# Three of four relus of the second mixture on ScalarE

## The chip, the cores and the metric

The kernel runs on one NeuronCore of a Trainium2 chip. A core has five engines that each work through a list of their own, in order: TensorE (PE in the profile, with its weight loads as PEld), VectorE (DVE), ScalarE (ACT), GpSimd (POOL) and SyncE (SP, which here issues DMAs). They wait for one another by semaphores. The metric is the device time of one execution in microseconds (us). Three runs of the kernel before gave 2256.85, 2263.62 and 2266.39 us, median 2263.62.

## The reference

For 32 sequences of 64 tokens with 256 channels, a first layer (a gated mixture of nine experts and a hyperbolic attention) is added to x. A second layer follows: the "second mixture" of dense networks named cond2, an attention with rotary positions, and a routed mixture of four experts. All is float32. The part that matters here, cut down:

```python
def _dense(x, wi_, wo_):
    return relu(x @ wi_) @ wo_
s0 = _dense(x, swi[0], swo[0])
s1 = _dense(x, swi[1], swo[1])
h  = relu(einsum('bsd,bdf->bsf', x, wi[type_label]))
eo = einsum('bsf,bfd->bsd', h, wo[type_label])
w  = softmax(relu(concat(eo[:,0], s0[:,0], s1[:,0]) @ g1) @ g2)
return eo * w[:,0] + s0 * w[:,1] + s1 * w[:,2]
```

Each token passes three dense networks of 256 to 1024 to 256, two shared and one chosen by the label of its sequence, and each of the three has a relu over its 1024 hidden values.

## The kernel before

The tokens are sorted into 16 tiles of 128, two tiles to a group, so there are eight groups. The first mixture takes the first part of the kernel. Then a loop `for k in range(1, GROUPS + 1)` (L1441) runs eight steps. Step k holds up to three pieces of work, written as Python generators and interleaved by `woven` (L1426): the hyperbolic attention of group k ("h", L396), the second mixture of group k-1 ("s", `selected`, L901), and the gate, rotary attention and routing of group k-2 ("r", L1322). The last step has the first weights of the routed mixture in place of "h". The routed mixture itself follows.

`woven` sets the order in which the instructions are written. The framework's planner then arranges them on each engine by its own estimate of when inputs are due, so a change of the engine of one instruction can also change the order of others. Once built, the order of every engine's list is fixed and it is kept at run time.

In `selected`, `dense` (L908) does four rounds: four matmuls of 128x256 (L917) fill one 128x512 bank of PSUM (`ph`, three buffers), and `relu` (L862) writes it to SBUF as `h`. Then sixteen matmuls (L931) bring the four `h` down to 256 channels. Each group runs this for the two shared networks. The chosen one is a third `dense` in groups 3 to 7, which hold one label each; in groups 0 to 2 it is made tile by tile, with two relus for each of two tiles (matmuls L969, transposes L984, matmuls L995). So every group has three fours of relus, 12 in all, and eight groups have 96.

`relu` counts its calls in `n_relu`. Odd calls run as an ACTIVATE on ScalarE (L866), even ones as a `tensor_scalar` maximum on VectorE (L868). In the first step (`first_step`) all twelve run on ScalarE.

Other lines that the prediction's steps touch:

- `hyperbolic`: exponentials L424 and L425, `u` L454, its transposes L294, keys `kb` L299, the scores L310, L464 and L465, square root L469, L472, logarithm L473, square L475, the mask L334.
- `attend`: row maxima L345, the subtraction on GpSimd L346, the exponential L347, transposes L354 with copies L356 (ScalarE) and L358 (VectorE), the product with the values L365, its sums L373, `y` L377, transposes L386, the copy L388, the output product L392.
- `gated_sum`: L1033, L1041, L1045, L1049, L1052, L1063, L1075, and the weighted sum L1082 to L1084.
- `rotary`: statistics L1096 and L1098, square root L1099, normalised rows `xn` L1102, transposes L1118, `pad` L1120, convolution `hc` L1132 and L1134, projection L267 and L270.
- SyncE's list: weights into `slot` (L875, L879), values into `vb` (L283).

Exponential, square root, logarithm and the gate of the first mixture need different function tables on ScalarE; each switch is an ACT_TABLE_LOAD in its list.

Of the kernel before, what the change touches and what calls it, by code (L numbers as in the profile page):

```python
# [76 lines left out]
def adaln_attn_ffn_kernel(ctx: ExitStack, tc: tile.TileContext, a, consts, out):  # L77
# [779 lines left out]
    n_relu = 0  # L857


    first_step = False  # L860

    def relu(dst, src):  # L862
        nonlocal n_relu
        n_relu += 1
        if n_relu % 2 or first_step:
            nc.scalar.activation(dst, src, AF.Relu)  # L866
        else:
            nc.vector.tensor_scalar(dst, src, 0.0, None, ALU.max)  # L868
# [32 lines left out]
    def selected(g, xT):  # L901
# [6 lines left out]
        def dense(w):  # L908

            hs = []  # L910
            for half in range(2):
                for pair in range(2):
                    ph = busy([P, 2, GN])
                    for k in range(2):
                        for c in range(2):
                            fc = 2 * pair + k
                            nc.tensor.matmul(  # L917
                                ph[:, k, :],
                                lhsT=w[half][:, c, fc * P : (fc + 1) * P],
                                rhs=xT[:, c, :],  # L920
                                start=c == 0,
                                stop=c == 1,
                            )
                    h = hidden([P, 2, GN])
                    relu(h, ph)
                    hs.append(h)
                    yield
# [31 lines left out]
        for k in range(NG if g < MIXED + PAIRS else 0):  # L959
# [5 lines left out]
            for half in range(2):  # L965
                ph = busy([P, 512])
                for c in range(2):
                    for b2 in range(P // width):
                        nc.tensor.matmul(  # L969
                            ph[b2 * width : (b2 + 1) * width, :],  # L970
                            lhsT=xT[:, c, k * P + b2 * width : k * P + (b2 + 1) * width],
                            rhs=w[b2][half][:, c, :],
                            start=c == 0,
                            stop=c == 1,
                        )
                h = hidden([P, 512])
                relu(h, ph)
                hs.append(h)
                yield
# [461 lines left out]
    for k in range(1, GROUPS + 1):  # L1441
# [11 lines left out]
        first_step = k == 1  # L1453
# [176 lines left out]
```

## Time and profile before

| | |
|---|---|
| three runs, median (us) | 2263.62 |
| the profiled execution's own time (us) | 2267.08 |
| its span, first to last instruction (us) | 2265.3 |
| PE busy in the span | 98% |
| DVE, ACT, POOL busy | 59%, 34%, 35% |
| mean granted TensorE clock | 0.994 |
| relus on ScalarE (L866), mean ns | 54, 590 |
| relus on VectorE (L868), mean ns | 42, 685 |
| first and last relu start (us from the span's start) | 1357.3, 2007.5 |

The profile names groups of instructions by their line, engine and tiles (out<-in). A group's row gives its busy time, the mean of one instruction in ns, and the idle time of the engine before them with what ended it. A row of the list of waits gives who waited, for whom, the total in us, how often, and the longest. A row of a table by stretches gives the busy time of each engine between two times and the clock that was granted to TensorE. A row of the timeline gives start, duration, engine, line, operation, and in square brackets the idle time before it and what ended it.

### The profile page before, as it was taken

The numbers are of one execution on the slowest core, as the hardware profiler recorded it, in microseconds if no ns is written. First come the engines' busy times: TensorE is split into PE (matmuls) and PEld (weight loads), VectorE is DVE, ScalarE is ACT, GpSimd is POOL, SyncE is SP. The second block draws the span as 40 slices with busy tenths as digits, with TensorE's granted clock in tenths as the row PEclk, the third lists the DMA queues.
The fourth block names the chain that finished last, engine by engine and source line by source line (L and its number), as shares of the span: only waits on it lengthen the run. The fifth ranks groups of instructions, "written<-read, shape, count | busy, mean of one in ns | idle before, by whom it ended". The sixth has DMA issues, their size and how long they took to land. (4 is left out here: it accounts for less than half of the span.)

```text
span 2265.3 us, 29780 instructions
## 1 busy us (share of the span) xinstructions
PE 2208.9 (98%) x11224; PEld 1801.3 (80%) x11224; DVE 1332.4 (59%) x2470; ACT 777.2 (34%) x1244; POOL 797.8 (35%) x693
## 2 busy tenths in 40 slices
PE   7999999999999999999999999999999999999998
PEld 6888888888888888888888786677687777766665
DVE  7465575565655756547565755767668668545222
ACT  2333333333333333333333544445245245222111
POOL 5653444454443545445354441122121221111110
PEclk9999999999999999999999999999999999999999
DMA  4010010190100101001000026443332322531110
GB/s 125 31 37 20 1 38 19 41 329 1 38 19 4 54 1 38 19 1 56 1 19 8 6 79 202 140 122 92 112 95 82 106 81 82 200 133 32 40 38 24
DMA packets 101470, 145.16 MB, mean 64 GB/s; under 512 B 10246, under 2 KB 63696, under 8 KB 101328
## 3 DMA queue, kind: packets, MB, share of 16 engines
q1 hardware_dynamic: 93056, 130.43, 18.0%
q0 software_dynamic: 3488, 10.00, 1.3%
q10 hardware_dynamic: 4784, 2.83, 0.4%
q8 instruction: 90, 1.47, 0.3%
q14 instruction: 52, 0.43, 0.1%
HBM read 114.67 MB, written 24.29 MB: 61 GB/s over the span
## 5 line engine op out<-in xcount | busy, mean ns | idle before, releaser
L677 ACT COPY cp<-X 128x512 f32<-128x512 f32 x432 | 251.3, 586 | 527.0 <-PE X L665 523.7
L685 DVE TENSOR_TENSOR cp<-W,cp 128x512 f32<-128x512 f32 x272 | 186.4, 690 | 86.2 <-ACT cp L677 71.4
L718 POOL TENSOR_TENSOR h_t<-h_t,h_b 128x512 f32<-128x512 f32 x72 | 95.0, 1319 | 349.0 <-DVE h_t L687 348.9
L686 ACT ACTIVATE cp<-cp 128x512 f32<-128x512 f32 x216 | 136.3, 631 | 226.3 <-DVE cp L685 226.2
L792 POOL TENSOR_TENSOR xg<-xT,mixw 128x1024 f32<-128x1024 f32 x36 | 71.2, 1978 | 325.9 <-PE W L665 309.2
L917 PE MATMUL ph<-xT,slot 128*128 128x256 f32 x672 | 167.4, 395 | 0.0
L931 PE MATMUL ph<-slot,h 128*128 128x256 f32 x672 | 161.0, 383 | 0.0
L685 DVE TENSOR_TENSOR cp<-Y,cp 128x512 f32<-128x512 f32 x160 | 109.9, 689 | 84.7 <-PE Y L665 77.0
L687 DVE TENSOR_TENSOR h_b<-cp 128x512 f32<-128x512 f32 x144 | 139.9, 972 | 19.3 <-ACT cp L686 3.3
L665 PE MATMUL X<-gS,w 128*128 128x256 f32 x576 | 148.1, 379 | 0.0
L665 PE MATMUL X<-xS,w 128*128 128x256 f32 x576 | 148.1, 380 | 0.0
L917 PEld LDWEIGHTS ph<-xT,slot 128*128 128x128 f32 x672 | 128.3, 197 | 16.9
L639 DVE TENSOR_TENSOR condT<-downA,condT 128x256 f32<-128x256 f32 x132 | 55.2, 419 | 141.3 <-PE downA L628 141.1
L931 PEld LDWEIGHTS ph<-slot,h 128*128 128x128 f32 x672 | 124.3, 191 | 16.3 <-issue 0.6
L628 PE MATMUL downA<-h_t,w 128*128 128x256 f32 x576 | 136.1, 379 | 0.0
L665 PEld LDWEIGHTS X<-gS,w 128*128 128x128 f32 x576 | 109.2, 190 | 15.4 <-issue 0.6
L628 PEld LDWEIGHTS downA<-h_t,w 128*128 128x128 f32 x576 | 109.4, 190 | 14.8
L665 PEld LDWEIGHTS X<-xS,w 128*128 128x128 f32 x576 | 109.0, 190 | 15.2 <-ACT cp L677 0.5
L639 DVE TENSOR_TENSOR condT<-downB,condT 128x256 f32<-128x256 f32 x104 | 43.4, 417 | 123.3 <-PE downB L628 123.3
L721 POOL TENSOR_TENSOR h_t<-h_b,h_t 128x512 f32<-128x512 f32 x72 | 111.5, 1549 | 0.0
L719 POOL TENSOR_TENSOR h_t<-h_b,h_t 128x512 f32<-128x512 f32 x72 | 105.2, 1461 | 4.2
L720 POOL TENSOR_TENSOR h_t<-h_b,h_t 128x512 f32<-128x512 f32 x72 | 95.7, 1329 | 0.0
(405 smaller groups left out, 4592.3 us busy)
## 6 DMA issues: line engine op xcount, KB each, us to landing
rows_d<-blank SPq DMA_DIRECT2D x67, 258.0 KB
slot<-in_L_cond_swi SPq DMA_DIRECT2D x32, 512.0 KB
slot<-in_L_cond_swo SPq DMA_DIRECT2D x32, 512.0 KB
slot<-in_L_cond_wi SPq DMA_DIRECT2D x26, 512.0 KB
slot<-in_L_cond_wo SPq DMA_DIRECT2D x26, 512.0 KB
w<-in_L_cond_Wg SPq DMA_DIRECT2D x8, 1024.0 KB
w<-in_L_cond_Wu SPq DMA_DIRECT2D x8, 1024.0 KB
w<-in_L_cond_Wd SPq DMA_DIRECT2D x8, 1024.0 KB
```

The costliest lines, as they stand in the source:

```text
L628: nc.tensor.matmul(po, lhsT=wd[l](q), rhs=h[q // 2][r][:, q % 2, :], start=fresh and q == 0, stop=q == Q - 1, skip_group_check=True,)
L639: nc.vector.tensor_tensor(acc, po, acc, ALU.add)
L665: nc.tensor.matmul(bank[m, name][:, k, :], lhsT=w[l][:, q * P : (q + 1) * P], rhs=src[r], start=fresh and k == 0, stop=True, skip_group_ch ...
L677: nc.scalar.copy(side[m, name], bank[m, "X"])
L685: nc.vector.tensor_tensor(t, bank[m, b], t, ALU.add)
L686: nc.scalar.activation(side["g", name], side["g", name], AF.Silu)
L687: nc.vector.tensor_tensor(h[key], side["g", name], side["u", name], ALU.mult)
L719: nc.gpsimd.tensor_tensor(h["t2"], h["b22"], h["t1"], ALU.subtract)
L720: nc.gpsimd.tensor_tensor(h["t3"], h["b22"], b12, ALU.subtract)
L721: nc.gpsimd.tensor_tensor(h["t4"], h["b21"], h["t2"], ALU.subtract)
L917: nc.tensor.matmul(ph[:, k, :], lhsT=w[half][:, c, fc * P : (fc + 1) * P], rhs=xT[:, c, :], start=c == 0, stop=c == 1,)
L931: nc.tensor.matmul(po[:, k, :], lhsT=hs[fc // 2][:, fc % 2, k * P : (k + 1) * P], rhs=w[2 + fc // 4][:, fc % 4, :], start=fc == 0, stop=fc ...
```

## The change

`n_relu % 2` becomes `n_relu % 4`. A call runs on VectorE only if its number divides by four and the first step is over.

```diff
     def relu(dst, src):
         nonlocal n_relu
         n_relu += 1
-        if n_relu % 2 or first_step:
+        if n_relu % 4 or first_step:
             nc.scalar.activation(dst, src, AF.Relu)
         else:
             nc.vector.tensor_scalar(dst, src, 0.0, None, ALU.max)
```

Each group makes twelve calls, so the count starts every group at a multiple of four: of each four, the second moves from VectorE to ScalarE, the fourth stays on VectorE. The first step has no relu on VectorE before or after. In the other seven steps 3 x 7 = 21 relus move: ScalarE has 75 and VectorE 21, where they had 54 and 42. Nothing else in the source changes. The planner arranges the lists of PE, VectorE and ScalarE anew around the moved relus; GpSimd's list stays the same, and SyncE's has one weight load and one register load in other places.

## The prediction

> **What bounds the kernel now.** I read the page's first part, then the groups by shape, the waits of PE, a table by stretches, and the timeline of step k = 5.
>
> ```profile
> span 2265.3 us, 29780 instructions
> ...
> PE 2208.9 (98%) x11224; PEld 1801.3 (80%) x11224; DVE 1332.4 (59%) x2470; ACT 777.2 (34%) x1244; POOL 797.8 (35%) x693
> ```
>
> PE is busy all but 2265.3 - 2208.9 = 56.4 us. The change touches no matmul, so time can only come from PE's idle time, or from its clock. The relus run from 1357 to 2008 us; in the stretch 1350 to 2010 PE is busy 634.28 of 660 us, so 25.7 us of idle time are at stake, and that includes step 1, which the change leaves alone.
>
> ```profile
> L866 ACT ACTIVATE h<-ph 128x512 f32<-128x512 f32 x54 | 31.8, 590 | 67.1 <-PE ph L917 49.9 <-PE ph L969 17.2
> ...
> L868 DVE TENSOR_SCALAR h<-ph 128x512 f32<-128x512 f32 x42 | 28.8, 685 | 15.3 <-PE ph L917 10.8 <-PE ph L969 4.4
> ```
>
> Both kinds of relu wait for PE. In the answers for these two lines, the waits of anyone for a relu sum to 1.3 us. The relus themselves are not late. What counts is what stands behind them on each engine. PE's own waits in steps 2 to 7 (1400 to 2000 us):
>
> ```profile
> PE at L267 <- DVE hc L1134: 6.2, 7, 0.9
> PE pt L354 <- ACT s L347: 5.3, 6, 0.9
> PE ph L1049 <- ACT h L1045: 2.1, 4, 0.6
> PE ph L1033 <- DMA vb<-v: 1.7, 2, 1.0
> PE pt L386 <- DVE y L377: 1.6, 4, 0.4
> ```
>
> The first is the end of a chain on VectorE, the second of one on ScalarE. They are nearly equal: the change takes from one and adds to the other. By stretches (columns: busy PE, PEld, DVE, ACT, POOL, then granted clock, DMA share, GB/s):
>
> ```profile
> 1510.00:1520.00 10.00, 8.45 (x42) 5.44 (x41) 5.72 (x16) 2.07 (x4) 2.07 (x2) 0.97 0.43 129
> 1520.00:1530.00 10.00, 10.00 (x45) 8.59 (x45) 7.58 (x37) 3.67 (x9) 0.00 (x0) 0.86 0.21 59
> 1600.00:1610.00 10.00, 8.17 (x38) 5.24 (x38) 5.87 (x17) 2.61 (x7) 2.07 (x2) 0.91 0.47 133
> 1610.00:1620.00 10.00, 10.00 (x32) 8.38 (x32) 4.97 (x26) 0.95 (x3) 0.00 (x0) 0.58 0.07 8
> 1640.00:1650.00 10.00, 10.00 (x68) 7.31 (x66) 9.73 (x17) 9.45 (x12) 1.53 (x2) 1.00 0.23 68
> ```
>
> Two things: in the middle of a step (last row) VectorE and ScalarE are both full, so ScalarE's 34% over the span says nothing there. And after stretches in which PE idled 1.55 and 1.83 us of ten, the clock fell, to 0.86 and 0.58.
>
> **The change, part by part.** 21 relus move. VectorE loses 21 x 685 = 14.4 us, ScalarE gains 21 x 590 = 12.4 us. On the end of the kernel only the place counts; there are three, each seven times. The built lists give the new order.
>
> *First four, near the start of the step.* VectorE in step 5:
>
> ```profile
> 1701.71 0.68 DVE L868 TENSOR_SCALAR h<-ph 128x512 f32<-128x512 f32 x1
> 1702.31 0.15 DVE L1076 TENSOR_REDUCE red<-wgt 128x2 f32<-128x6 f32 x1
> ```
>
> The next instruction starts 0.60 us later, and VectorE then has hardly a gap up to `xn` (L1102), whose transposes lead to `pad`, `hc` and PE's wait at L267:
>
> ```profile
> 1710.03 0.33 PE L1118 MATMUL pt<-ident,xn 128*128 128x128 f32 x1 [0.23 <-DVE xn L1102]
> ...
> 1714.60 1.98 PE L267 MATMUL at<-w_qkv,hc 128*128 128x512 f32 x4 [0.89 <-DVE hc L1134]
> ```
>
> So `hc` comes 0.60 us earlier. But the new list of PE puts 17 matmuls of the mixture between L1063 and this L267 (apart from the first twelve) where there were 18, in steps 2, 5, 6, 7; one is 0.43 us (eight records of L931 from 1710.96 to 1712.69, two to a matmul), and it has to be made up later. Net gain 0.60 - 0.43 = 0.17 each. In step 4 it is 12 in place of 14: 0.60 - 0.86 = -0.26. In steps 3 and 8 the count stays: 0.60 each. Together 4 x 0.17 - 0.26 + 2 x 0.60 = 1.6 us gained. On ScalarE this relu now stands ahead of the second exponential (L425): it starts when its matmuls end, near 1701.7, so L425 ends near 1702.5 where it ended at 1701.28. VectorE asks for it at 1706.79 (L444): hidden by 4 us of other VectorE work; without that cover 1.2 us a step.
>
> *Second four, inside the full stretch.* The relu goes in ScalarE's list ahead of the logarithm's table load, where a relu takes 0.48 us (first two rows, start to start):
>
> ```profile
> 1733.56 0.58 ACT L866 ACTIVATE h<-ph 128x512 f32<-128x512 f32 x1
> 1734.04 1.04 ACT L475 ACTIVATE za<-za 128x1024 f32<-128x1024 f32 x1
> 1736.62 0.59 ACT L356 COPY sT<-pt 128x512 f32<-128x512 f32 x1 [1.53 <-PE pt L354]
> ```
>
> The 1.53 us gap ahead of L356 takes it up: nothing. The mask (L334) that waits for the square has been put later in VectorE's list. VectorE's keys (L299) may start 0.6 us earlier; PE shows no wait for them between 1400 and 2000 us (its weight loads do, ahead of time, beside running matmuls). Without the gap: 7 x 0.48 = 3.4 us.
>
> *Third four, at the end of the stretch.* On VectorE in step 5 the relu stood at 1740.44, ahead of L472 and then `y` (L377). In the new list `y` stands ahead of L472 and the relu is gone: PE's wait for `y`, 1.6 us in all, ends. On ScalarE the moved relu stands behind the exponentials `s` that PE waits for. But L472 now comes behind `y`, whose start-to-start cost is 0.33 us (L377 at 1743.15, next at 1743.48), and the chain L472, logarithm, square, exponential leads to PE's wait for `s`. From below, the 0.60 us saved more than pays for it and the wait of 5.3 us ends; from above, the chain is late by the two earlier relus too, 6 x (0.33 + 0.48) = 4.9 us. I take 6 x 0.33 = 2.0 us, as `y` is the one row that is known to have moved ahead.
>
> *Table loads.* Both built lists hold 103 loads (1283 ns each in the profile) at the same lines; the 54 relus of before have none of their own. Nothing. *SyncE.* In step 4 one weight load (issued at 1643.40) now stands behind four `vb` issues of 2.38 us; in the whole trace one wait for a slot shows, 0.5 us of a weight load (L969): nothing. The register load near the end moves by tenths.
>
> *The clock.* By the rows above, the loss is (1 - 0.97 + 1 - 0.86) x 10 = 1.7 us near step 3 and 5.1 us near step 4; two like it, 1940 to 1960 and 2020 to 2040, cost 1.7 each. I leave it as it is, and give it to the range.
>
> Sum: -1.6 - 1.6 + 2.0 = -1.2 us. Against the profiled execution, 2267.08 - 1.2 = 2265.9; that one lies 3.46 above the median of the runs, so on their scale 2263.62 - 1.2 = 2262.4, say **2262**.
>
> [...] The rows here have 590 ns on ScalarE and 685 on VectorE, in float32 out of PSUM. [...]
>
> **Rivals.** *Slower: ScalarE's chain becomes the bound.* In the full stretch the gap of 1.53 us vanishes because PE comes earlier with L354, so both moved relus reach PE's wait for `s`: 7 x 2 x 0.6 = 8.3 us, and the longer gap drops the clock in four of seven steps, 4 x 1.7 = 6.8. With the 1.2 saved: +14, or 2278. For: ScalarE is busy 9.45 of ten us there. Against: the relu of the third four is listed behind `s`. It decides once a step's wait for `s` grows by over 1.6 us, clock included. *Faster: VectorE was the real bound.* The waits for `hc` shrink by 7 x 0.60 = 4.2, `y` goes (1.6), `xn` (0.7) and L995 (0.9) too, and with fewer gaps the clock stays up near steps 3 and 4 (6.8) and at 1940 (1.7): -15.9, or 2248. For: VectorE 9.73 of ten. Against: the falls near steps 3 and 4 follow waits for DMA and ScalarE (L1033, L1049), which the change does not shorten.
>
> **How the numbers follow.** Within 0.5% (11.3 us, about what a measurement of this kernel can tell from no change; the three runs lie 9.5 apart): 0.58, own range 2254 to 2271. Slower 0.24, faster 0.18. The range reaches into both rivals until about a tenth is left out at each end: 2249 to 2280.
>
> **What would show it.** 75 relus at L866 near 590 ns, 21 at L868; PE's wait for `hc` at 4 to 6 us, for `y` near nothing, for `s` 6 to 8; 103 table loads; clock falls of similar sum. Wrong if PE's waits for ScalarE grow by over 10 us, or if the clock row falls in more steps, or in none.

## The result, and the profile after

The changed kernel takes 2265.74 us (median of 20 runs, 2262.0 to 2267.83); the kernel before, run beside it, 2260.47 (20 runs, 2256.85 to 2266.39). The ratio is 1.0018, 95% interval 1.0012 to 1.0025: 4.1 us slower. The forecast was 1.2 us faster; the time lies inside its range, but on the other side of no change. That 2265.74 lies only 3.7 us from the forecast 2262 is in part luck: the three runs that it started from had a median 3.2 us above that of the twenty.

The first part of the changed kernel's page, and the two relu lines from its list of groups:

```profile
span 2263.1 us, 29799 instructions
...
PE 2206.4 (97%) x11224; PEld 1796.7 (79%) x11224; DVE 1324.1 (59%) x2449; ACT 789.0 (35%) x1265; POOL 797.9 (35%) x693
...
L866 ACT ACTIVATE h<-ph 128x512 f32<-128x512 f32 x75 | 44.3, 594 | 65.1 <-PE ph L917 45.0 <-PE ph L969 17.1 <-issue 2.9
...
L868 DVE TENSOR_SCALAR h<-ph 128x512 f32<-128x512 f32 x21 | 14.2, 677 | 9.6 <-PE ph L917 8.2 <-PE ph L969 1.4
```

The 21 relus moved and kept their durations. But the span is shorter than the 2265.3 us shown of before, and PE is busy for less. That misleads, and the reason is the clock. Here are stretches of the changed kernel's table (columns as before: PE, PEld, DVE, ACT, POOL, granted clock, DMA share, GB/s):

```profile
1520.00:1530.00 10.00, 10.00 (x52) 8.66 (x51) 8.88 (x39) 4.07 (x9) 0.00 (x0) 1.00 0.41 112
1610.00:1620.00 10.00, 10.00 (x49) 8.45 (x47) 8.64 (x30) 2.77 (x4) 1.66 (x2) 1.00 0.32 107
...
1940.00:1950.00 10.00, 8.40 (x52) 6.82 (x51) 2.42 (x10) 3.04 (x5) 0.14 (x1) 0.85 0.91 321
```

The falls to 0.86 and 0.58 that the first trace had near 1525 and 1615 us are absent. Eight records of L917 at the end of step 3 take 3.76 us in that trace, from 1609.18 us, across its stretches at 0.91 and 0.58, and 1.97 us here, from 1606.37 us, at 1.00. Over 1350 to 2040 us, (1 - clock) times the stretch sums to 12.0 us in that trace and to 5.1 us here. How often the clock falls differs from run to run: the runs of the kernel before with a mean clock of 0.994 took 2264.7 us on average (21 runs), those with 0.996 took 2259.8 (39 runs), those with 0.997 took 2258.3 (51 runs; all of these ran beside the experiments below). The first trace had 0.994. At 0.996 the changed kernel took 2265.4 (12 runs): 5.6 us more at one and the same clock.

So the two traces have to be compared in stretches where the clock held. I cut the loop at the start of each step's first L1063 and took the table by these stretches. First steps 4, 5 and 6 of a second trace of the kernel before (run f0 below), then of the changed kernel:

```profile
1612.00:1695.29 83.29, 81.55 (x539) 64.31 (x538) 58.49 (x138) 35.24 (x51) 19.34 (x20) 1.00 0.30 91
1695.29:1780.15 84.86, 82.15 (x539) 64.14 (x538) 60.98 (x147) 36.81 (x56) 19.33 (x20) 1.00 0.29 91
1780.15:1864.77 84.62, 81.91 (x539) 64.23 (x538) 60.25 (x147) 36.82 (x56) 15.94 (x16) 1.00 0.28 88
```

```profile
1608.18:1695.10 86.92, 81.69 (x539) 64.06 (x538) 57.28 (x136) 36.80 (x54) 19.34 (x20) 1.00 0.27 87
1695.10:1780.62 85.52, 83.08 (x539) 64.34 (x538) 59.91 (x144) 38.30 (x59) 19.40 (x20) 1.00 0.30 91
1780.62:1865.98 85.36, 83.10 (x540) 64.34 (x539) 59.59 (x144) 38.31 (x59) 15.98 (x16) 1.00 0.29 88
```

There are two kinds of loss. Step 4 is 3.6 us longer with PE no busier: waits, 5.2 us where 1.7 were. Steps 5 and 6 (and 7: 80.96 against 80.27) are 0.7 us longer each, with PE 0.9 to 1.2 us *busier* on the same matmuls, and waiting 0.3 to 0.5 us less. Together 3.6 + 0.66 + 0.74 + 0.69 = 5.7 us, near the 5.6 of the runs at equal clock. Steps 2 and 3 can't be compared so, since both traces of before have clock falls in them; the run e1 below, which has TensorE's old list and no fall there, takes 88.57 and 87.98 us for them, the changed kernel 87.98 and 87.90: no loss.

PE's waits between 1400 and 2000 us after the change:

```profile
PE at L267 <- DVE hc L1134: 6.2, 7, 0.9
PE pt L354 <- ACT s L347: 5.4, 6, 1.9
...
PE at L365 <- DVE sT L358: 1.5, 2, 1.2
...
PE at L392 <- ACT yT L388: 0.9, 4, 0.2
```

The wait for `y` is gone. The wait for `s` has its old sum, but its longest is now 1.9 us. L365 and L392 are new.

### The profile page after: what moved, and what is told of

Same layout as the page of the kernel before. It is cut to its first block, busy times and chain, and to the rows that moved or that the text cites. A ratio compares the mean times of both kernels' runs of the same rounds, so it can differ in the third digit from the quotient of the medians.

```text
span 2263.1 us, 29799 instructions
## 1 busy us (share of the span) xinstructions
PE 2206.4 (97%) x11224; PEld 1796.7 (79%) x11224; DVE 1324.1 (59%) x2449; ACT 789.0 (35%) x1265; POOL 797.9 (35%) x693
## 5 line engine op out<-in xcount | busy, mean ns | idle before, releaser
L917 PE MATMUL ph<-xT,slot 128*128 128x256 f32 x672 | 163.8, 388 | 0.0
L931 PE MATMUL ph<-slot,h 128*128 128x256 f32 x672 | 160.9, 383 | 0.2
L931 PEld LDWEIGHTS ph<-slot,h 128*128 128x128 f32 x672 | 123.6, 191 | 17.9 <-ACT h L866 2.2
L917 PEld LDWEIGHTS ph<-xT,slot 128*128 128x128 f32 x672 | 125.0, 193 | 15.7
```

The lines of the kernel that those rows point to most:

```text
L917: nc.tensor.matmul(ph[:, k, :], lhsT=w[half][:, c, fc * P : (fc + 1) * P], rhs=xT[:, c, :], start=c == 0, stop=c == 1,)
L931: nc.tensor.matmul(po[:, k, :], lhsT=hs[fc // 2][:, fc % 2, k * P : (k + 1) * P], rhs=w[2 + fc // 4][:, fc % 4, :], start=fc == 0, stop=fc ...
```

## The experiments

The planner gave TensorE a new list with the change. To tell the relus from that list, its order can be held: in the changed or the old source each matmul of steps 2 to 7 gets an ordering dependency on the one before it in a list that I choose. This fixes an order within one engine and asks for no wait on another; but the planner may place a few instructions of other engines differently around it. No run holds the changed kernel's own list unaltered; h1, which holds it with a few places moved, has 1.0016 where the free one has 1.0018. The edit is the same in all of the runs with a held list, so below only the list is given. It moves their line numbers by 100 (103 in g2, 119 in i1, 122 in i3).

```diff
+    traced = {i.name: i for i in nc.cur_bb.bb.instructions}
+    queue = [traced["I-" + n] for n in PE_ORDER.split()]
+    for prev, ins in zip(queue, queue[1:]):
+        tc.add_manual_dep(
+            ins, prev.name, mybir.DependencyInfo(mybir.DependencyClass.NoSync, mybir.DependencyReason.DATA), reason="pinned"
+        )
```

All results: the ratio to the kernel before, run beside it; the difference in us at equal clock (each run against the mean of the 148 runs of before that had the same mean clock; f0 shows that 1 us is nothing here; some runs of e2 and one of f2 had a clock that before never had, and are left out); lengths of steps from one trace each, first L1063 to first L1063. f2's and i3's step 4 contain clock falls, to 0.60 and to 0.84 in stretches of 10 us, as do step 5 of e2 and g4 (mean clock 0.98); h2's step 6 contains a wait of 1.0 us for a DMA (L1033).

| run | ratio, 95% interval | us at equal clock | step 4 | step 5 | step 6 | step 7 |
|---|---|---|---|---|---|---|
| f0, before again | 1.0002 (0.9991 to 1.0014) | +0.9 | 83.29 | 84.86 | 84.62 | 80.27 |
| the change | 1.0018 (1.0012 to 1.0025) | +5.5 | 86.92 | 85.52 | 85.36 | 80.96 |
| e1 | 1.0008 (0.9999 to 1.0017) | +0.5 | 83.57 | 84.29 | 84.34 | 79.99 |
| e2 | 1.0063 (1.0043 to 1.0082) | +7.1 | 86.67 | 87.12 | 85.57 | 81.41 |
| e3 | 1.0005 (0.9996 to 1.0013) | +1.0 | 83.66 | 84.64 | 84.44 | 80.27 |
| e4 | 1.0011 (1.0004 to 1.0017) | +2.5 | 85.08 | 84.15 | 84.56 | 79.78 |
| f1 | 0.9994 (0.9984 to 1.0004) | +1.3 | 83.57 | 85.06 | 84.98 | 80.96 |
| f2 | 1.0019 (1.0007 to 1.0031) | +4.4 | 93.19 | 84.42 | 84.22 | 80.00 |
| f3 | 1.0053 (1.0038 to 1.0068) | +12.5 | 85.67 | 86.42 | 86.12 | 82.03 |
| g1 | 0.9999 (0.9989 to 1.0008) | +2.1 | 83.90 | 84.54 | 84.31 | 79.97 |
| g2 | 1.0015 (1.0002 to 1.0027) | +1.4 | 85.41 | 84.31 | 84.21 | 79.99 |
| g3 | 1.0011 (1.0002 to 1.0020) | +3.0 | 86.55 | 84.34 | 84.30 | 79.99 |
| g4 | 1.0026 (1.0014 to 1.0037) | +3.3 | 84.03 | 86.55 | 85.98 | 81.50 |
| h1 | 1.0016 (1.0007 to 1.0025) | +4.9 | 86.33 | 85.33 | 85.39 | 81.32 |
| h2 | 1.0000 (0.9990 to 1.0011) | +2.1 | 83.58 | 85.34 | 86.39 | 81.33 |
| i1 | 0.9982 (0.9972 to 0.9991) | -3.0 | 83.89 | 84.15 | 84.35 | 80.08 |
| i2 | 0.9993 (0.9983 to 1.0003) | -1.1 | 83.60 | 84.50 | 84.42 | 80.36 |
| i3 | 0.9989 (0.9980 to 0.9998) | -1.4 | 85.85 | 84.17 | 84.17 | 80.08 |

**Is it the relus or the new list?** e1 has the relus of the change and TensorE's list of before; e2 is the mirror image.

> The 21 relus on ScalarE as in the changed kernel, but TensorE's list held in the order of the kernel before for steps 2 to 7. Theory A (TensorE's new order costs about 1 us a step in finer pieces of small matmuls, and the moved relus themselves cost nothing): back to the kernel before, ratio 0.9990 to 1.0007. Theory B (the moved relus lengthen ScalarE's chains): as slow as the changed kernel or slower, 1.0012 to 1.0030. Theory C (only the clock of TensorE differs from run to run): no expectation on the time, but the runs with full clock agree with the kernel before.

> The relus on the engines of the kernel before, but TensorE's list held in the order of the changed kernel. Theory A: slower by the whole difference or more, 1.0013 to 1.0035 (4 to 8 us), with TensorE's busy time up by about 1 us a step. Theory B: no slower than 1.0008.

e1's 1.0008 lies between the two forecasts, and its interval takes in parts of both, no change among them; so the traces have to decide. Its steps 5 to 7 are shorter than before, and its row of waits for `s` is the old one, 5.3 us: with the old list the relus on ScalarE do not lengthen the chain up to `s` in any way that PE sees. One small mark of theirs is there, a wait of 0.30 us at L365 in step 4 that before does not have. e2 is slower than either theory had it, the slowest of all, and for a reason of its own:

```profile
PE ph L1031 <- DVE h L968: 7.3, 4, 1.8
```

L931 (1031 here) waits for relus on VectorE that the new list asks for too early. The new list fits the new engines only, so e2 can't price the list by itself.

**One four at a time.** Lists were left to the planner.

```diff
-        if n_relu % 2 or first_step:
+        if n_relu % 2 or n_relu % 12 == 6 or first_step:     # e3: the second fours
+        if n_relu % 2 or n_relu % 12 == 2 or first_step:     # e4: the first fours
```

> Only the second relu of the second four moves to ScalarE (7 relus in place of 21); the planner then leaves TensorE's list as it was. Theory A: 0.9993 to 1.0007. Theory B: a third of the loss or more, since this is the place inside ScalarE's full stretch: +1.3 to +3.4 us, 1.0006 to 1.0015.

> Only the second relu of the first four moves (7 relus); the planner changes TensorE's list in other places than in the changed kernel. Theory A: the time follows the number of switches between kinds of matmuls in the new list, which its trace will show, 0.9995 to 1.0020. Theory B: this place is outside ScalarE's full stretch, so 0.9990 to 1.0003.

e3 moves one relu in three, TensorE's list stays, and nothing measurable happens; but its interval also takes in the lower part of what theory B expected, so that it decides little. e4 makes the planner move matmuls, and costs 1.1 parts in a thousand, with step 4 at 85.1 us, where B expected at most 0.3. That speaks for the list.

**Step 4, and the price of alternating.** f0 is the kernel before without an edit.

> The kernel before once more, as a measure of what no change looks like and for a second trace. Every theory: ratio 1.000 within 0.001. If the trace shows no clock fall between 1480 and 1700 us, step 4 (between the L1063 of two steps) should take about 83.6 us and not 86.1, and steps 5, 6, 7 again 84.8, 84.9 and 80.3 us: the 86 to 90 us of steps 2 to 4 in the first trace were then its clock's and not the kernel's.

It came out as expected: 83.29 us for step 4, without the fall of the clock at its start that the first trace had.

```diff
 PE_ORDER (relus as in the change)
-steps 2, 3, 5, 6, 7: as the change    step 4: as the change
+steps 2, 3, 5, 6, 7: as the change    step 4: as before     # f1
+steps 2, 3, 5, 6, 7: as before        step 4: as the change # f2
```

> Relus as in the changed kernel, TensorE's list as in the changed kernel in steps 2, 3, 5, 6, 7, but as before in step 4. Theory A1 (step 4's order is most of the loss: 5.2 us of waits there where 2.0 are usual): step 4 falls from 86.9 to about 83.7 us, the others stay at 85.5, 85.4, 81.0, and the ratio to the kernel before is 1.0018 - 3.2/2260 = 1.0004. Theory A2 (the finer pieces in steps 2, 5, 6, 7 are the loss): ratio stays near 1.0018.

> The mirror image: relus as in the changed kernel, TensorE's list as before everywhere but in step 4, which has the order of the changed kernel. A1: step 4 at about 86.9 us, steps 5, 6, 7 at 84.3, 84.3, 80.0 as in the run with the old list throughout; ratio 1.0008 + 3.2/2260 = 1.0022. A2: step 4 costs nothing by itself, ratio 1.0008.

Both ratios came out as A1 has it, f1's with help from the clock. Restoring step 4 takes the loss away (0.9994), and putting it alone into the old list brings it back (1.0019). f1's steps 5, 6 and 7 keep their longer times, yet f1 isn't slower than before: its runs had a mean clock of 0.997, those of before 0.9955. At equal clock f1 is 1.3 us slower than before, so step 4 is 4.2 of the 5.5 us.

```diff
 PE_ORDER, steps 2 to 7 (relus as in the change, the rest as before)
-L310 x16, L354 x8
+L310 x12, then L354 and L310 in turns four times, L354 x4    # f3
```

> Relus as in the changed kernel, TensorE's list as before, but in steps 2 to 7 the last four scores matmuls (L310) and the first four transposes behind them (L354) of the hyperbolic attention take turns, where they stood as 4 and then 4 of a kind: eight changes of kind more in each of two places or one place per step, 8 x 6 = 48 in all counted in the lists. If a change of kind costs TensorE what the trace of the changed kernel shows (0.307 us L310 to L354 and 0.331 back, against 0.09 and 0.116 within a kind, so 0.216 each), 48 x 0.216 = 10.4 us: ratio 1.0008 + 10.4/2260 = 1.0054, with PE's idle time unchanged and its busy time up. If a change of kind costs nothing and the loss is all waits or clock: 1.0008.

Expected 1.0054, measured 1.0053. The table's row for step 5, first e1 and then f3:

```profile
1692.45:1776.73 84.28, 81.85 (x539) 64.21 (x538) 59.52 (x144) 38.61 (x59) 19.33 (x20) 1.00 0.30 92
```

```profile
1699.61:1786.03 86.42, 84.24 (x540) 64.80 (x538) 59.19 (x144) 38.63 (x59) 19.36 (x20) 1.00 0.29 90
```

The same matmuls, eight more changes of kind, and PE is busy for 2.39 us more; the step is 2.14 us longer, 0.27 us for each. The timeline of f3 has the turns one by one (L310 and L354 are L410 and L454 there):

```profile
1735.56 0.33 PE L454 MATMUL pt<-ident,s 128*128 128x128 f32 x1
1735.82 0.64 PE L410 MATMUL at<-kb,qT 64*64 64x256 f32 x2
1736.39 0.33 PE L454 MATMUL pt<-ident,s 128*128 128x128 f32 x1
```

From one L454 to the next 0.83 us, where these three records within their own kinds take 0.29 (in e1, 32 records of L310 in 2.89 us, and 0.11 for an L354): 0.54 more for two changes.

**Which changes cost: of kind, or of tile?** The column ahead of the sizes is the tile: 64*64 for L310, 128*64 for L365, 128*128 for nearly all else. g1 alternates two kinds with the same tile.

```diff
 PE_ORDER, steps 2 to 7 (relus as in the change, the rest as before)
-L392 x4, L917 x4
+L917 and L392 in turns four times      # g1 (L984 in steps 2 and 3)
```

> Relus as in the changed kernel, TensorE's list as before, but in steps 2 to 7 four matmuls of the second mixture (L917, or L984 in steps 2 and 3) and the four of the output product L392 take turns, where they stood as 4 and 4: 36 more changes of kind in all, none of them a change of tile, since all these matmuls have tiles of 128*128. Theory T (what costs is the change of tile, 128*128 to 64*64 or 128*64 and back): busy time of steps 5, 6, 7 stays at 81.9, 81.9, 76.2 us and the ratio at 1.0008. Theory K (any change of kind costs 0.216 us): 36 x 0.216 = 7.8 us, ratio 1.0042.

```profile
1696.23:1780.77 84.54, 82.03 (x539) 64.24 (x538) 59.70 (x144) 38.49 (x59) 19.37 (x20) 1.00 0.30 92
```

Busy 82.03 us against e1's 81.85, and the ratio is 0.9999: theory T. The changes of kind within one tile cost next to nothing, at most 0.3 us of busy time for the six of a step (81.83 us against 81.54 in step 4); a change of tile, 128*128 to 64*64 or back, cost 0.27 us in f3, and one to or from 128*64 was not measured by itself. (g1's step 3 is 1.3 us longer than e1's, 89.25 against 87.98, mostly by waits.) The change raised the number of changes between these three tiles from 10 to 16 in steps 5, 6 and 7, and from 12 to 16 in step 2.

**What happens in step 4?** ScalarE and PE in step 4 of the changed kernel:

```profile
1646.93 1.85 PE L365 MATMUL at<-vb,sT 128*64 128x34 f32 x32 [1.22 <-DVE sT L358]
...
1650.54 0.38 PE L386 MATMUL pt<-ident,y 128*128 128x128 f32 x2
...
1650.96 0.37 ACT L388 COPY yT<-pt 128x256 f32<-128x256 f32 x1 [1.61 <-PE pt L386]
1651.35 1.28 ACT L473 ACT_TABLE_LOAD   x1
...
1657.17 0.66 PE L354 MATMUL pt<-ident,s 128*128 128x128 f32 x4 [1.92 <-ACT s L347]
```

The new waits of this step are 1.22 us at L365, 1.07 more than before at L354, 0.55 at L1214, 0.36 at L310 and 0.29 at L1033: 3.5 us. The small copy L388 stands ahead of the logarithm's table load and waits 1.61 us for PE; logarithm, square and the exponential `s` are late behind it. g2 is f2 with two pairs of ScalarE's list exchanged:

```diff
 ScalarE's list, step 4 (TensorE's list as in f2)
-L388, load, L473, load, L347, L475
+load, L473, L388, L475, load, L347     # g2
```

> The kernel with TensorE's list as before except in step 4, where it is the changed kernel's; the only further edit is on ScalarE in step 4: the copy L388 stands behind the logarithm L473 and its table load where it stood ahead of the load, and the square L475 ahead of the exponential L347 where it stood behind. If the late copy (which waits 1.6 us for TensorE with the logarithm's load behind it) is what makes the second long wait of step 4, TensorE's wait at L354 falls from 1.9 us to at most 0.9 and the step gets 1.0 to 1.9 us shorter, while the wait at L365 stays at 1.2: ratio 1.0019 - 1.5/2260 = 1.0012. If TensorE's own order makes it, nothing changes: 1.0019.

```profile
1650.30 1.28 ACT L576 ACT_TABLE_LOAD   x1
...
1651.47 0.38 PE L489 MATMUL pt<-ident,y 128*128 128x128 f32 x2
...
1653.01 0.35 ACT L491 COPY yT<-pt 128x256 f32<-128x256 f32 x1
...
1656.84 0.66 PE L457 MATMUL pt<-ident,s 128*128 128x128 f32 x4
```

The load starts while PE is still on its way to the transposes of `y`, and the waits at L354 (457) and L1214 no longer show. Step 4 is 1.5 us shorter than in the changed kernel, though its first 1.26 us had a clock of 0.69; PE's idle time in it falls from 5.2 to 3.1 us. The ratio, 1.0015, is near the 1.0012 expected, though its interval takes in f2's 1.0019 too; at equal clock g2 is 3.0 us faster than f2. The first wait, at L365, stays.

```diff
 PE_ORDER, step 4 (the rest of it as in f2)
-L931 x6, L1118 x4, L931 x6, L267 x2, L270 x2, L931 x4, L294 x8, L917 x2,
-L310 x16, L267 x2, L270 x2, L917 x6
+L931 x7, L1118 x1, L931 x1, L1118 x3, L931 x6, L267 x2, L270 x2, L931 x2, L917 x2, L294 x8, L917 x2,
+L310 x16, L267 x2, L270 x2, L917 x4    # g3: the early part as before
```

The whole early part is the old one again, with two L931 back ahead of L267 beside the pair of L917.

> The kernel with TensorE's list as before except in step 4, where it is the changed kernel's; but the early part of step 4 has one pair of matmuls L917 back ahead of the scores L310, and with it the relu that reads them stands ahead of the exponential L347, in ScalarE's idle 3.8 us, and no longer directly ahead of the logarithm's load. If that relu is what makes the first long wait, TensorE's wait at L365 falls from 1.2 to about 0.7 us (one relu of 0.49 us less on the chain), the 0.36 us at L310 goes, and step 4 is 0.8 us shorter; the wait at L354 stays near 1.9: ratio 1.0019 - 0.8/2260 = 1.0015. Otherwise 1.0019 and the same waits.

Only in part. L365 waits 0.92 us and not 0.7, the 0.36 us at L310 stay, a wait of 0.46 us at L294 is new, and step 4 is 86.55 us: 0.4 us gained, not 0.8. L365 does start 0.49 us earlier after L267 than in the changed kernel (25.30 us, 25.79 there), as much as the relu that no longer runs ahead of the logarithm. But PE gets there earlier too: this list has 21 matmuls of the mixture between L267 and L365, the old one 24.

The traces show what stands behind this wait. `sT` (L358) comes behind the mask L334 on VectorE, and the mask waits for the square L475. Step 4 before (f0):

```profile
1642.40 1.28 ACT L473 ACT_TABLE_LOAD   x1
...
1646.21 1.22 DVE L334 SCALAR_TENSOR_TENSOR za<-za,cst 128x1024 f32<-128x1024 f32 x1
```

and in the changed kernel, with two relus directly ahead of that load:

```profile
1637.72 1.10 ACT L866 ACTIVATE h<-ph 128x512 f32<-128x512 f32 x2
...
1638.84 1.28 ACT L473 ACT_TABLE_LOAD   x1
...
1642.65 1.23 DVE L334 SCALAR_TENSOR_TENSOR za<-za,cst 128x1024 f32<-128x1024 f32 x1 [1.09 <-ACT za L475]
```

e1 and g3 have one relu there. In both, L365 starts 25.30 us after L267, but e1, with 24 matmuls of the mixture in between, waits 0.30 us for it and g3, with 21, 0.92. Read so, the 1.22 us are 0.3 for the first relu, 0.6 for three matmuls fewer ahead, and 0.3 for the second relu. The split is read from traces, not tested by a run of its own.

**An attempt that failed.** g4 puts more work ahead of the wait for `hc`.

```diff
 PE_ORDER, steps 4 to 7 (relus as in the change, the rest as before)
+two more matmuls of the mixture ahead of L267, all later ones two places earlier    # g4
```

> An attempt at something better than both: relus as in the changed kernel, TensorE's list as before, but in steps 4 to 7 two more matmuls of the second mixture stand ahead of the projection L267, and two fewer of them in the run of L931 ahead of L392 late in the step, where TensorE does not wait; all in between move up by two. If the wait for hc (0.89 us in each step) is only a matter of filling, it falls to about 0.03 us and each of four steps is 0.9 us shorter: ratio 1.0008 - 3.5/2260 = 0.9993. If the waits are set by chains that now find less work beside them elsewhere, they come back at L354 or L294 and the ratio stays at 1.0008.

The wait for `hc` goes in these steps, and another takes its place:

```profile
PE ph L1031 <- ACT h L966: 5.9, 3, 2.0
```

Three waits of 2.0 us for relus on ScalarE, which the shifted L931 (1031) now ask for before they are made; a rival that I hadn't listed. (In its step 5 a clock fall took some 1.7 us besides.)

**Do the extra tile changes cost the changed kernel anything?**

```diff
 PE_ORDER, steps 2, 5, 6, 7 (all else as the change in h1; step 4 as before in h2)
-L310 x12, L354 x1, L310 x4, L354 x7
+L310 x16, L354 x8
-L365 x4, L917 x2, L354 x8, L917 x2, L354 x4, L365 x16, L917 x1, L365 x12
+L917 x2, L354 x8, L917 x2, L354 x4, L365 x32, L917 x1
```

> The changed kernel, with its own list on TensorE but for one thing: in steps 2, 5, 6 and 7 the one L354 in the middle of sixteen L310 goes behind them, the four L365 that stand alone join the other sixteen, and the one L917 (L969 in step 2) among these goes behind them. Each of these steps then has 10 changes of tile (12 in step 2) where the changed kernel has 16. If a change of tile costs what the alternating run showed (0.2 to 0.3 us): busy time of steps 5, 6, 7 falls from 83.1, 83.1, 77.4 to about 81.9, 81.9, 76.2; the four L365 no longer fill the wait at L354, which grows by about 0.4 us; so 0.8 us in each of four steps, 3.2 us: ratio 1.0018 - 0.0014 = 1.0004. If the tiles cost nothing in the time: 1.0018 or more.

> The same with the order of step 4 as before the change, so that both losses found are gone and the moved relus stay. If the tiles cost: 0.9994 - 0.0014 = 0.9980, faster than both kernels. If they do not: 0.9994. If shorter waits and fewer clock falls were what held that run at 0.9994, merging gives them back and it ends near 1.0008 as the run with the old list throughout.

Little or nothing: h1's 1.0016 is what was expected if the tiles cost nothing, and h2's 1.0000 lies between its second and third case. PE's busy time in step 5 falls by 0.71 us (82.37), but its wait at L354 grows from 0.64 to 1.43 us, that at L310 to 0.40, and the steps keep their length within 0.4 us. The fine pieces were what filled the wait for `s`. So the question is why `s` is late.

**VectorE's list.** Step 5 in the first trace of the kernel before:

```profile
1738.66 0.68 DVE L358 COPY sT<-pt 128x512 f32<-128x512 f32 x1
...
1739.26 1.27 DVE L345 TENSOR_REDUCE mx<-za 128x8 f32<-128x512 f32 x2
...
1741.18 0.63 ACT L347 ACTIVATE za<-za 128x512 f32<-128x512 f32 x1
...
1741.42 0.26 DVE L373 RECIPROCAL inv<-at 128x16 f32<-128x16 f32 x1 [0.29 <-PE at L365]
...
1747.38 1.14 ACT L347 ACTIVATE s<-s 128x512 f32<-128x512 f32 x2
```

and in the changed kernel, whose step begins 3.72 us earlier:

```profile
1733.52 0.69 DVE L358 COPY sT<-pt 128x512 f32<-128x512 f32 x1
1734.12 1.22 DVE L334 SCALAR_TENSOR_TENSOR za<-za,cst 128x1024 f32<-128x1024 f32 x1
...
1736.55 0.26 DVE L373 RECIPROCAL inv<-at 128x16 f32<-128x16 f32 x1 [1.22 <-PE at L365]
1736.72 0.63 DVE L345 TENSOR_REDUCE mx<-za 128x8 f32<-128x512 f32 x1
...
1738.60 0.63 ACT L347 ACTIVATE za<-za 128x512 f32<-128x512 f32 x1 [1.73 <-POOL za L346]
...
1744.66 1.13 ACT L347 ACTIVATE s<-s 128x512 f32<-128x512 f32 x2
```

The mask L334 has gone behind L358, and the row maxima L345 behind the reciprocal L373, which waits 1.22 us for PE. GpSimd's subtraction, the exponential, the logarithm and `s` follow: `s` starts 48.56 us into the step before (1747.38 - 1698.82) and 49.56 after (1744.66 - 1695.10), 1.0 us later. In i1, i2 and i3 the maxima go first; nothing is changed in TensorE's list.

```diff
 VectorE's list, steps 2, 5, 6, 7
-L334, L373, L345, L377, L472
+L334, L345, L373, L345, L377, L472
 i1: TensorE's list as in f1     i2: as in h2
 i3: as in the change, and ScalarE's list in step 4 as in g2
```

(The second maxima in the new order is one that stood behind L472; the planner moved it up.)

> The run with step 4's old order (f1), and in steps 2, 5, 6 and 7 the row maxima L345 stand ahead of the reciprocal L373 on VectorE. Theory V (the maxima behind a reciprocal that waits 1.22 us make s late): s comes about 1.0 us earlier, TensorE's wait at L354 (0.65 us) goes, each of four steps is 0.6 us shorter (85.06, 84.98, 80.96 to about 84.4, 84.4, 80.4): ratio 0.9994 - 2.4/2260 = 0.9983, faster than both kernels. Theory P (TensorE's order sets the wait): no change, 0.9994.

> The same edit on the run with the tiles merged and step 4's old order (h2), whose wait at L354 is 1.43 us. V: that wait falls to about 0.4 us, each of four steps is 1.0 us shorter: ratio 1.0000 - 4/2260 = 0.9982. P: no change, 1.0000.

> The changed kernel with its own list on TensorE throughout. On VectorE the maxima L345 stand ahead of L373 in steps 2, 5, 6, 7; on ScalarE in step 4 the logarithm stands ahead of the copy L388 and the square ahead of the exponential. V, and the finding on step 4: 1.0018 - (2.4 + 1.5)/2260 = 1.0001, the loss is gone with TensorE's list untouched. P: 1.0018 - 0.7/1000 = 1.0011 at best.

i1 in step 5 (L345 is L464 there, L373 is L492, L347 is L466, L354 is L473):

```profile
1733.33 0.69 DVE L464 TENSOR_REDUCE mx<-za 128x8 f32<-128x512 f32 x1
...
1734.51 0.26 DVE L492 RECIPROCAL inv<-at 128x16 f32<-128x16 f32 x1 [0.50 <-PE at L484]
...
1735.26 0.63 ACT L466 ACTIVATE za<-za 128x512 f32<-128x512 f32 x1 [0.43 <-POOL za L465]
...
1742.40 0.66 PE L473 MATMUL pt<-ident,s 128*128 128x128 f32 x4 [0.25 <-ACT s L466]
```

The reciprocal's wait now passes behind the maxima, and PE's wait for `s` falls from 0.64 to 0.25 us. The ratio is 0.9982 where 0.9983 was expected. i1 beats both kernels: its slowest run, 2258.64, is faster than the fastest of the changed kernel. i2 gains less (0.9993 where 0.9982 was expected), since without the fine pieces 1.03 us of the wait remain (0.4 was expected). i3 shows the cause: TensorE's list is the changed kernel's to the last matmul, and with the lists of two other engines mended the ratio goes from 1.0018 to 0.9989, by more than the 3.9 us expected (6.6; 6.9 at equal clock). In its step 4 the wait at L354 no longer shows, and those at L310 and L365 stay.

## Why the prediction was wrong

**Its premise on PE was wrong.** "The change touches no matmul, so time can only come from PE's idle time, or from its clock." The matmuls are the same, but their order isn't, and busy time depends on it: 0.9 to 1.2 us more in each of steps 5 to 7. I read the new list for how many matmuls stand ahead of L267 and not for its tiles. As h1 shows, this term alone cost the time next to nothing net; it hid the wait that the next point is about.

**The step that failed is the one on the second four and the mask.** It put the mask's later place at "nothing" because a gap on ScalarE took the relu up. For the relu that held in step 5: the gap ahead of L356 fell from 1.53 to 1.24 us. (In step 4 it did not: there the relus ahead of the logarithm's load reach PE by the mask, as shown above.) But on VectorE the mask pushed the row maxima behind the reciprocal, and `s` is 1.0 us late in each of steps 2, 5, 6 and 7. The step on the third four looked at the right chain and the right queue but priced the wrong neighbour: it charged L472 for standing behind `y` (six times 0.33 us). To bring `y` forward its reciprocal L373 had to come forward as well, with its wait for PE, and ahead of L345. The question that I asked of `y`, "what stands behind it?", was not asked of the reciprocal.

**Step 4 was assumed to be like step 5.** Only its count of matmuls ahead of L267 was worked out, and put at 0.26 us. Its own order on ScalarE (L388 and two relus ahead of the logarithm) and on TensorE cost 3.6 us, the larger part of the loss. f1 and f2 show that it is there, g2 that the copy's place is at least 1.5 us of it; the split of the rest is read from traces.

**The first four was mis-sized.** Forecast -1.6 us. L267 starts 0.50 us earlier in step 5, with one matmul fewer ahead of it (0.43): 0.07 gained, where 0.17 was put. In step 3 it is 0.11 us and not 0.60 (13.85 to 13.74 us into the step), in step 4 -0.12. Over steps 2 to 7 that is 0.3 us; in step 8 a longer clock fall hides it (from 1940 to 1960 us 3.4 us of clock, 1.7 in the first trace). The wait for `hc` kept its 6.2 us.

**What held.** `y` no longer keeps PE waiting (-1.6), though 0.9 us at L392 came in its place. Both kernels have the same table loads; the relu of the third four stands behind `s`. The wait for `s` did not rise to 6 to 8 us but kept 5.4, since the fine pieces filled it. The relus kept 594 and 677 ns (590 and 685 before), and their own time shows, as far as I read the traces, only in step 4's wait at L365, by some 0.6 us.

**The rivals.** "ScalarE's chain becomes the bound" got its side and its wait right for step 4, but the two relus are the smaller part of it: with PE's old list (e1) they cost 0.3 us in step 4 and nothing in steps 5 to 7. (Its sum has a slip: 7 x 2 x 0.6 is 8.4, not 8.3.) "VectorE was the real bound" had part of the truth: with VectorE freed and the maxima first, i1 is 3.0 to 4 us faster than before. How much of that the freed relus give by themselves was not measured.

**The clock.** It was left as it is. The two traces of before lost 12.0 and 8.5 us to it between 1350 and 2040 us, that of the change 5.1. In the runs that is a mean clock of 0.9960 against 0.9958 (the 148 runs of before beside the experiments), so it took nothing away and gave some tenths of a us. The slower rival's sum had a longer gap drop the clock in four of seven steps; in the changed kernel's trace PE idled 1.92 us of the ten from 1650 to 1660 us, more than ahead of the falls that the prediction shows, and the clock stayed at 1.00 there and in the next ten.

**Open:** why e1, whose steps 5 to 7 are 0.3 to 0.6 us shorter than those of before, is not faster in its runs, at equal clock either; and what makes the 0.36 us at L310 in step 4. i1's gain over f1 (1.2 parts in a thousand) is not the clock's: i1's was lower, 0.9966 against 0.9971.

## What to carry to other kernels

If a planner orders the lists, moving one instruction to another engine means new lists on all of them: compare the lists of every step, also those that look like copies of each other, before pricing the instruction. In each list ask of every instruction that came forward what it waits for, and what critical work stands behind it; a 0.26 us reciprocal or a 0.37 us copy ahead of the long chain cost more here than the 21 relus did with the old list (e1). And compare traces in stretches with the same granted clock: here the slower kernel had the shorter span.

## What the runs showed of the hardware

A change of TensorE's tile (128*128 to 64*64 or back) cost 0.27 us of the step in f3's trace, 0.21 by its ratio, and showed as busy time, not as a wait (84.24 us in step 5 where e1 has 81.85); a change between different kinds of matmuls with one tile added at most 0.3 us of busy time for six of them (48 of the first: ratio 1.0008 to 1.0053; 36 of the second: 1.0008 to 0.9999).

The granted clock fell, to 0.86 and 0.58 in stretches of 10 us near 1525 and 1615 us of the first trace; the longest wait of PE near the second was 0.97 us. Which stretches it met differed between two traces of one kernel (1610 to 1620 us: 0.58 in one, 0.92 in the other), and of the 148 runs of before the 11 with a mean clock of 0.993 took 2265.8 us on average, the 51 with 0.997 took 2258.3. Nor did equal waits bring equal falls: step 4 of f2 has the changed kernel's waits at L365 and L354 (1.2 and 1.9 us); its trace has the clock at 0.83 in each of the two stretches of 10 us from 1650 to 1670, while the changed kernel's kept 1.00 through its step 4.
